# One fused Mamba-and-attention kernel: the scan's state copies and due times, the split of products over the engines, and the last image's end

## The chip, the cores and the metric

The kernel runs on one core of one Trainium2 chip. The metric is the device time of one execution in microseconds (us); the median over several executions is compared. A core has five engines with queues of their own, which wait for each other by semaphores: TensorE (PE, matrix products and transposes; PEld is its weight load), VectorE (DVE), ScalarE (ACT), GpSimd (POOL) and SyncE (SP, which here only issues DMAs). SBUF is the on-chip memory of 128 partitions, PSUM the accumulator memory that PE writes; POOL's operands here all lie in SBUF.

## What is computed

Two layers over x of shape 4 x 512 x 32 x 32 (float32), each after a group normalization and added to its input:

```python
# layer 0, per image: L = 1024 tokens, d_inner = 1024, 16 states
xn = layernorm(tokens(gn(x))) * ln_w + ln_b
xm, z = split(xn @ W_in)
xs = silu(causal_conv4(xm) + conv_b)
proj = xs @ W_x                          # 32 dt columns, 16 B, 16 C
dt = softplus(proj[..., :32] @ W_dt + b_dt)
def step(h, inp):
    dA = jnp.exp(dt_t[..., None] * A)
    h = dA * h + (dt_t * x_t)[..., None] * B_t[:, None, :]
    y = jnp.einsum('bds,bs->bd', h, C_t)
    return (h, y)
x1 = x + ((scan(step) + xs * D_param) * silu(z)) @ W_out
# layer 1, per image, on g = gn(x1)
top, center = conv1x1(g, w_top), conv1x1(g, w_center)     # 64 channels
bottom = conv3x3(g, w_bottom)
att = softmax over all of (center^T top) @ bottom
out = x1 + conv3x3(g + att, w_out)
```

## The kernel before

**Scan stage (layer 0).** The 1024 channels are eight chunks of 128 (`d`), the 1024 tokens two halves of 512 (`h`). For each image `b`, each pair of chunks `e` and each half `h` there are 16 *units*, one for each state `s`: 4 x 4 x 2 x 16 = 512 units. A unit (`unit`, L726 and behind) does, for its two chunks `j`:

- exp(dt * A) on ACT (L746), the *decay*;
- dt * x * B. For the states of `B_ON_ACT` ACT scales the transposed dt * x by B (four instructions of 128 x 256, L758, into a tile `sc`, two buffers) and PE turns it back into PSUM (L784, eight transposes, into a tile `u`, four buffers). For the others POOL multiplies 128 x 1024 by a row of B that SP has broadcast (`bbc`, L767 and L773);
- the recurrence along 512 tokens as one DVE scan for each chunk (L798), from `carry_sb` in the second half;
- in the first half a copy of the last column into `carry_sb`. For the states of `C_ON_DVE`, whose scan writes PSUM, it is inside the scan's step, one number per partition (L803). For the others it is a step of its own behind both scans, two numbers per partition from SBUF (L820);
- the product with C: on POOL, both chunks at once, in place (L826), or on DVE for `C_ON_DVE` (L814), by a row of C that SP has broadcast (`cbc`, L739, six buffers);
- the sum over states: PE transposes the product into PSUM, accumulating (L833).

At the end of 16 units comes a gate (L856 to L876). Between the units lie: for the next image the normalization, the projections with four-tap convolution (`pxm`; L601 on ACT, L610 on DVE), `params` (x times W_x, 16 matmuls, L652) and `delta` (dt, dtx L710 and its transpose); the gates' projections `pz`; the output projection `po`, which writes x1 to DRAM; and 32 transforms of the 3 x 3 convolution weights for layer 1, on POOL and ACT, which fill gaps.

**What sets the order.** All steps of layer 0 are handed to `Plan`. A step has an engine, an estimated time and a due time `prio`, counted in units (one image is 128 units). `Plan.issue` plays the steps through on estimated clocks: among the steps of an engine that could start within `SLACK` of the earliest, it takes the one with the least due time, and no step further than `AHEAD` units in front of the oldest one left. The result is the fixed instruction order of each engine. `PRM` holds the due times: `m0`, `n0`, `nl` normalization of the next image, `q0`/`qg` start and step of its eight x projections for the second image and `c0`/`cg` for later ones, `p0` params, `dl` how far ahead of its units a delta is due, `e0`/`eg` and `g0`/`gg` gates, `o0`/`og` output projection, `t0`/`tg` weight transforms, `fi` the first image's load for layer 1.

**Layer 1.** Not planned by hand: the framework's scheduler orders it. For each image: `scores`, the first 3 x 3 convolution (`conv3`, called b), `attend`, which adds the attention to the padded image `xg`, the second `conv3` (called o) and `finish`. `conv3` takes its weights from DRAM in 24 pieces of 1 MB (L1385, three buffers) through 192 matmul instructions (L1389), in three pairs of points; each point takes four products q = 2, 1, 0, 3. ACT and DVE combine them into `n` (L1397, L1405), and POOL adds `n` to `y[0]` and `y[3]` behind the last pair (L1409, L1410). `finish` loads x1 (L1463, three buffers), turns y back on PE (L1470), adds on DVE (L1475) and stores (L1480). The two bias rows `brow` are loaded and scaled on ACT at the start of layer 1 (L1195, L1198). In the last image the first pair's input of conv o is made chunk by chunk inside `attend`.

Of the kernel before, what the change touches and what calls it, by code (L numbers as in the profile page):

```python
# [29 lines left out]

PRM = dict(fi=4.61, m0=27.7, n0=50.77, nl=1.39, q0=50.1, qg=7.76, c0=53.17, cg=7.07, p0=120.48, e0=6.38, eg=3.72, g0=78.98, gg=9.04, o0=14.48, og=4.13, dl=9.01, t0=10, tg=21.42)

# [23 lines left out]
class Plan:  # L56
# [4 lines left out]
    LAG = {"PE": 0.2, "DVE": 0.08, "ACT": 0.1, "POOL": 0.06, "SP": 0.0}  # L61
    HOP, LOAD, SLACK, AHEAD = 0.05, 1.3, 0.05, 17.64

# [106 lines left out]
def mamba_then_pab_kernel(  # L170
# [46 lines left out]
    nc.gpsimd.dma_start(pb_sb[PAB:P], b_center)  # L217

    def padded(b, pool, tag):

        xg = pool.tile([P, NCC, HH + 2, WW + 2], F32, tag=tag, name=f"xg_{b}")
        nc.gpsimd.memset(xg[:, :, 0, :], 0.0)
        nc.gpsimd.memset(xg[:, :, HH + 1, :], 0.0)
        nc.gpsimd.memset(xg[:, :, 1 : HH + 1, 0], 0.0)
        nc.gpsimd.memset(xg[:, :, 1 : HH + 1, WW + 1], 0.0)
        return xg
# [37 lines left out]
    with ExitStack() as l0:  # L264
# [12 lines left out]

        B_ON_ACT = (0, 2, 4, 6, 7, 8, 10, 12, 14, 15)

        C_ON_DVE = (1, 6, 11)  # L280

# [39 lines left out]
        def dram_set(name, shape, n=B):  # L321
# [7 lines left out]
        slots = {  # L329
            "xt": 1, "xs": 10, "win": 2, "yt": 1, "dt": 2, "dtx": 2, "dtxt": 2, "cbc": 6,  # L330
            "sc": 2, "h": 4, "sz": 1, "bb": 3, "dbx": 4, "szl": 1, "wpr": 2, "res": 2,
# [28 lines left out]
        bts = [buf(None, bt_sb[k], "") for k in range(2)]  # L360
        carry = [buf(None, None, "") for s in range(NS)]
        bcds = [buf(None, t, "") for t in bcd]
# [280 lines left out]
        def params(b, prio):  # L643

            p0 = b % 2 * NP
            pr = proj[b % 2]
            for h, hs in enumerate(halves):
                pp = buf("mm" if b else f"y{h}", [P, T], f"pp_{b}_{h}")
                for d in range(NDC):
                    step(  # L650
                        "PE", MM,
                        lambda d=d, hs=hs, pp=pp: nc.tensor.matmul(  # L652
                            pp()[p0 : p0 + NP, :], wx_sb[:, d, :], xs[b, d]()[:, hs],
                            start=(d == 0), stop=(d == NDC - 1),
                        ),
                        [xs[b, k] for k in range(NDC)] if b and d == 0 else [xs[b, d]], [pp],
                        prio if b else prio - 10 + d + 0.5,
                    )
                step(
                    "ACT", 0.48,  # L660
                    lambda hs=hs, pp=pp: nc.scalar.copy(pr()[:, hs], pp()[p0 : p0 + NP, :]),
                    [pp], [pr], prio,
                )
            step(
                "SP", 0.3, lambda: nc.sync.dma_start(bcd[b], pr()[RK:NP, :]),
                [pr], [bcds[b]], prio, kb=128,
            )
            pt = buf("mm", [P, NT, NP], f"pbt_{b}")

            def turn():  # L670
                for k in range(NT):
                    nc.tensor.transpose(
                        pt()[:, k, :], pr()[:, k * P : (k + 1) * P],
                        ident[p0 : p0 + NP, p0 : p0 + NP],
                    )

            step("PE", 8 * TR, turn, [pr], [pt], prio)
            bt = bts[b % 2]
            step(
                "DVE", 0.21, lambda: nc.vector.tensor_copy(bt(), pt()[:, :, RK : RK + NS]),  # L680
                [pt], [bt], prio,
            )
# [45 lines left out]
        def unit(b, e, h, s, y):  # L728
# [15 lines left out]
            def decay(j, t):  # L744
                at = (2 * e + j) * NS + s
                nc.scalar.activation(t, dt()[:, j], AF.Exp, scale=a_sb[:, at : at + 1])  # L746
# [31 lines left out]
            for j, u in enumerate(us):  # L778
                part = parts[j]
                if on_act:  # L780

                    def turn(j=j, u=u):
                        for k in range(NK):
                            nc.tensor.transpose(  # L784
                                u()[:, k * P : (k + 1) * P], sc()[:, k, j, :], ident
                            )

                    step(
                        "ACT", EXP, lambda j=j: decay(j, hc()[:, j]), [dt], [part], prio, "exp",
                        holds=[hc],  # L790
                    )
                    step("PE", 4 * TR, turn, [sc], [u], prio - 1)
                else:
                    step("ACT", EXP, lambda j=j, u=u: decay(j, u()), [dt], [u], prio - 1, "exp")

                def scan(j=j, u=u):
# [4 lines left out]
                    )  # L801
                    if h == 0 and on_dve:
                        nc.vector.tensor_copy(carry_sb[:, j, s : s + 1], ht[:, T - 1 : T])  # L803

                before, behind = ([carry[s]], []) if h else ([], [carry[s]] if on_dve else [])
                step(
                    "DVE", SCAN + (0.15 if behind else 0.0), scan,
                    [part if on_act else hc, u, *before],
                    [u if on_dve else part, *behind], prio - 1, holds=[hc],
                )  # L810
                if on_dve:
# [4 lines left out]
                    )  # L816
            if h == 0 and not on_dve:
                step(
                    "DVE", 0.15,
                    lambda: nc.vector.tensor_copy(carry_sb[:, :, s], hc()[:, :, T - 1]),  # L820
                    parts, [carry[s]], prio - 1, holds=[hc],
                )
            if not on_dve:
# [5 lines left out]
            for j in range(2):  # L829
# [8 lines left out]

                step("PE", 4 * TR, add, [parts[j]], [y[j]], prio, holds=[hc])

# [149 lines left out]
        def first_image(prio):  # L990
# [10 lines left out]

            step("POOL", 1.2, make, [], [pieces, *chunks], prio)
            for c in range(NCC):
                for h in range(NH):
# [6 lines left out]
                        ),  # L1011
                        [x1s[0][h]], [chunks[c]], prio, kb=512,
                    )
# [161 lines left out]
    with ExitStack() as l1:  # L1175
# [14 lines left out]


        brow = []
        for name, src in (("b", b_bottom), ("o", b_out)):
            t = wp.tile([1, C], F32, tag=f"brow_{name}", name=f"brow_{name}")
            nc.scalar.dma_start(  # L1195
                t.rearrange("o (c p) -> o c p", p=P), src.rearrange("p (c o) -> o c p", o=1)
            )
            nc.scalar.activation(t, t, AF.Copy, scale=2.0 / ALPHA[1])  # L1198
            brow.append(t)
        NMC = L // P  # L1200
# [116 lines left out]

        def conv3(name, xg, u, bias, first=None):

# [46 lines left out]
            for pair in PAIRS:  # L1366
# [14 lines left out]
                for k, p in enumerate(pair):  # L1381
                    m = {}
                    for q in (2, 1, 0, 3):
                        w = fp.tile([P, NCC, C], F32, tag="u", name=f"uw_{name}_{p}_{q}", bufs=3)
                        nc.sync.dma_start(w, u[q][p])  # L1385
# [13 lines left out]
                    for o, src, w, add, op in (  # L1399
# [5 lines left out]
                        nc.vector.scalar_tensor_tensor(o, src, w, add, ALU.mult, op)  # L1405
                    ns.append(n)

                if pair == (0, 5):
                    nc.gpsimd.tensor_add(y[0], y[0], ns[0])  # L1409
                    nc.gpsimd.tensor_add(y[3], y[3], ns[1])  # L1410
                    break
                a, d = (
# [17 lines left out]
        def attend(b, xg, st, rp, xb, between, chunk):  # L1430


            for k in range(NCC * NH):
# [20 lines left out]
                if h and chunk:  # L1454
                    chunk(j)

        def finish(b, y):

            dst = out[b].rearrange("(c p) h w -> p c (h w)", p=P)
            for j in range(NCC):  # L1460
                o = fp.tile([P, L], F32, tag="f4", name=f"o_{b}_{j}")
                for h in range(NH):
                    nc.sync.dma_start(  # L1463
                        o[:, h * T : (h + 1) * T], x1[b][h][j * P : (j + 1) * P, :]
                    )
                ov = o.rearrange("p (i r j k) -> p r k i j", r=4, j=TJ, k=2)
                for rr in range(2):
                    pt = ps.tile([P, 4, P], F32, tag="ps", name=f"po_{b}_{j}_{rr}")
                    for k in range(4):
                        nc.tensor.transpose(  # L1470
                            pt[:, k, :], y[2 * rr + k // 2][:, k % 2, j * P : (j + 1) * P], ident
                        )
                    for k in range(2):
                        o2 = ov[:, 2 * rr + k]
                        nc.vector.tensor_add(  # L1475
                            o2, o2, pt[:, 2 * k : 2 * k + 2].rearrange(
                                "p k (i j) -> p k i j", j=TJ
                            ),
                        )
                nc.scalar.dma_start(dst[:, j, :], o)  # L1480

        xg = image[0]
        st, rp = scores(0, xg)
        for b in range(B):
# [5 lines left out]
            attend(b, xg, st, rp, xb, after, chunk)  # L1490
            if b + 1 < B:
                st, rp = scores(b + 1, image[b + 1])
            finish(b, conv3(f"o{b}", xg, uo, brow[1], v))
            xg = image.get(b + 1)
# [57 lines left out]
```

## Time and profile before

| | us |
|---|---|
| median of 3 runs | 3147.45 (3142.55 to 3149.4) |
| the profiled execution | 3152.2 |
| its span | 3150.4 |

| engine | busy us in the span | share |
|---|---|---|
| PE | 2801.1 | 89% |
| DVE | 2324.9 | 74% |
| ACT | 1896.9 | 60% |
| POOL | 2185.6 | 69% |

The scan stage runs from about 120 to 2096 us, layer 1 from about 2123 to the end. The shares over the whole span mix the two: layer 1 uses POOL and ACT little. In group lines the columns are line, engine, operation, what is written from what, shape and count, then busy us and the mean ns of one, then the engine's idle time in front of them and who ended it. In a timeline line they are start and length in us, engine, line, operation, and in brackets the idle time in front. A window line has the stretch, its length, and for each engine the busy us and the number of instructions.

### The profile page before, as it was taken

To read this page: it belongs to the slowest core of one execution; us is meant where nothing else is said; L and a number is where in the kernel's file an instruction comes from. 1 tells how busy PE (TensorE), PEld (TensorE's weight loads), DVE (VectorE), ACT (ScalarE), POOL (GpSimd) and SP (SyncE) were. 2 spreads that over 40 slices of the span, in tenths; PEclk is the share of its full clock that TensorE was granted. 3 is DMA by queue.
4 is the path that set the end of the run, shared out by engine and by line. 5 is a ranking of instruction groups with operands and counts; after the bars stand their busy time and mean duration, and the time that the engine had idled before them with its cause. 6 is when DMAs were issued, how large, how long until landed. Compare 5 with 4: busy or idle time off the path is not lost. (4 is left out here: it accounts for less than half of the span.)

```text
span 3150.4 us, 36613 instructions
## 1 busy us (share of the span) xinstructions
PE 2801.1 (89%) x11832; PEld 1654.8 (53%) x11832; DVE 2324.9 (74%) x2746; ACT 1896.9 (60%) x3322; POOL 2185.6 (69%) x1207
## 2 busy tenths in 40 slices
PE   4988878989888999888999877779999999999998
PEld 2455656666556656565655655544444444444443
DVE  3488899988999988999987987876275366447344
ACT  3499889998799999789998787752030030020000
POOL 8899898999969999978899998853052142224222
PEclk8999899999999999999999989989999999999999
DMA  6666455577645567745567654457268448628817
GB/s 190 192 186 195 144 152 162 156 226 241 212 118 169 163 204 250 231 114 155 165 192 227 204 172 123 121 139 263 93 225 312 183 147 317 257 74 312 321 61 253
DMA packets 401414, 600.03 MB, mean 190 GB/s; under 512 B 47176, under 2 KB 241992, under 8 KB 376648
## 3 DMA queue, kind: packets, MB, share of 16 engines
q1 hardware_dynamic: 392128, 582.13, 58.8%
q10 hardware_dynamic: 8936, 15.31, 1.3%
q8 instruction: 94, 1.54, 0.2%
q14 instruction: 96, 0.79, 0.1%
q0 software_dynamic: 160, 0.26, 0.0%
HBM read 500.60 MB, written 96.99 MB: 190 GB/s over the span
## 5 line engine op out<-in xcount | busy, mean ns | idle before, releaser
L826 POOL TENSOR_TENSOR da<-da,cbc 128x1024 f32<-128x1024 f32 x288 | 679.4, 2364 | 87.2 <-DVE carry_sb L820 47.4
L758 ACT ACTIVATE sc<-dtxt,bt_sb 128x256 f32<-128x256 f32 x1280 | 557.1, 496 | 49.3 <-PE u L784 48.8
L746 ACT ACTIVATE da<-dt,a_sb 128x512 f32<-128x512 f32 x640 | 439.4, 713 | 70.1 <-PE y L833 69.5
L773 POOL TENSOR_TENSOR dbx<-dtx,bbc 128x1024 f32<-128x1024 f32 x192 | 452.1, 2367 | 30.6 <-DMA bbc<-bcd 8.3
L784 PE MATMUL u<-ident,sc 128*128 128x128 f32 x2560 | 380.6, 282 | 52.4 <-DVE da L798 31.7
L833 PE MATMUL y<-ident,da 128*128 128x128 f32 x2560 | 357.3, 283 | 70.7 <-POOL da L826 68.2
L798 DVE TENSOR_TENSOR_SCAN da<-da,carry_sb,u 128x512 f32<-128x512 f32 x288 | 353.3, 1260 | 82.8 <-PE u L784 82.6
L833 PEld LDWEIGHTS y<-ident,da 128*128 128x128 f32 x2560 | 297.6, 145 | 183.4 <-POOL da L826 134.2
L784 PEld LDWEIGHTS u<-ident,sc 128*128 128x128 f32 x2560 | 302.2, 144 | 160.3 <-issue 41.7
L798 DVE TENSOR_TENSOR_SCAN da<-da,u 128x512 f32<-128x512 f32 x288 | 337.1, 1202 | 37.3 <-PE u L784 37.2
L1389 PE MATMUL m_b<-uw_b,v_b 128*128 128x512 f32 x768 | 339.1, 599 | 10.3 <-DMA uw_b<-u_b 9.4
L1389 PE MATMUL m_o<-uw_o,v_o 128*128 128x512 f32 x768 | 333.5, 595 | 4.3 <-DVE v_o L1311 4.1
L826 POOL TENSOR_TENSOR dbx<-dbx,cbc 128x1024 f32<-128x1024 f32 x128 | 302.8, 2365 | 32.1 <-DVE carry_sb L820 22.6
L381 PE MATMUL pxm<-xt,winc 128*128 128x344 f32 (+2 forms) x768 | 249.6, 469 | 30.5 <-DVE xs L610 13.9
L746 ACT ACTIVATE u<-dt,a_sb 128x512 f32<-128x512 f32 x384 | 252.9, 679 | 34.8 <-DVE da L798 18.9
L833 PE MATMUL y<-ident,dbx 128*128 128x128 f32 x1536 | 217.1, 281 | 43.7 <-POOL dbx L826 31.6
L381 PE MATMUL pz<-xt,winc 128*128 128x512 f32 x512 | 246.2, 599 | 10.5 <-ACT sz L631 3.1
L1389 PEld LDWEIGHTS m_b<-uw_b,v_b 128*128 128x128 f32 x768 | 144.7, 191 | 197.8 <-issue 185.7
L1389 PEld LDWEIGHTS m_o<-uw_o,v_o 128*128 128x128 f32 x768 | 145.5, 190 | 190.5 <-issue 181.2
L833 PEld LDWEIGHTS y<-ident,dbx 128*128 128x128 f32 x1536 | 178.4, 144 | 98.2 <-POOL dbx L826 48.6
L1437 PE MATMUL pat<-y_b,st 128*128 128x512 f32 x512 | 221.7, 593 | 0.1
L1397 ACT ACTIVATE e_b<-m_b 128x512 f32<-128x512 f32 x24 | 14.3, 596 | 320.6 <-PE m_b L1389 299.4
(231 smaller groups left out, 4536.2 us busy)
## 6 DMA issues: line engine op xcount, KB each, us to landing
cbc<-bcd SPq DMA_DIRECT2D x512, 256.0 KB, 3.7
uw_b<-u_b SPq DMA_DIRECT2D x96, 1024.0 KB, 4.9
uw_o<-u_o SPq DMA_DIRECT2D x96, 1024.0 KB, 4.9
bbc<-bcd SPq DMA_DIRECT2D x192, 256.0 KB, 4.1
u_b<-work SPq DMA_DIRECT2D x192, 128.0 KB, 2.3
u_o<-work SPq DMA_DIRECT2D x192, 128.0 KB, 3.1
winc<-in_w_in_dram SPq DMA_DIRECT2D x64, 256.0 KB, 3.8
szd<-sz SPq DMA_DIRECT2D x32, 512.0 KB, 3.6
```

The lines of the kernel that those rows point to most:

```text
L381: lambda k=k, lhs=lhs, rhs=rhs: nc.tensor.matmul(p()[:, at : at + cols], lhs(), rhs(), start=(k == 0), stop=(k == n - 1)),
L746: nc.scalar.activation(t, dt()[:, j], AF.Exp, scale=a_sb[:, at : at + 1])
L758: nc.scalar.activation(sc()[:, k], dtxt()[:, k], AF.Copy, scale=bt()[:, at, s : s + 1])
L773: lambda: nc.gpsimd.tensor_mul(hc(), dtx(), b_bc().to_broadcast([P, 2, T])),
L784: nc.tensor.transpose(u()[:, k * P : (k + 1) * P], sc()[:, k, j, :], ident)
L798: nc.vector.tensor_tensor_scan(ht, *((hc()[:, j], u()) if on_act else (u(), hc()[:, j])), carry_sb[:, j, s : s + 1] if h else 0.0, ALU.mul ...
L826: lambda: nc.gpsimd.tensor_mul(hc(), hc(), c_bc().to_broadcast([P, 2, T])),
L833: nc.tensor.matmul(y[j]()[:, k, :], hc()[:, j, k * P : (k + 1) * P], ident, start=(s == 0 and k == 0), stop=(s == NS - 1 and k == NK - 1), ...
L1389: nc.tensor.matmul(m[q], v[:, q, k, c, :], w[:, c, :], start=(c == 0), stop=(c == NCC - 1 and not extra),)
L1397: nc.scalar.activation(e, m[2], AF.Copy, scale=al / 2)
L1437: nc.tensor.matmul(pt, st[m][:, 2 * P * j + h : 2 * P * (j + 1) : 2], xb[m // 2][:, m % 2, :], start=(m == 0), stop=(m == NMC - 1),)
```

## The change

In the scan stage the copy of the state is made in each scan's step, one number per partition, for every state. `B_ON_ACT` loses state 7 (nine states on ACT), `C_ON_DVE` becomes (1, 5, 9, 13) from (1, 6, 11). The turns L784 are due two units ahead (`kt`), the accumulating transposes L833 0.68 units later (`ka`), the 16 params matmuls one every 0.53 units from 112 (`pg`, `p0`), and other due times move; `ke` and `fl` have the values that leave things as they were. `cbc` has five buffers instead of six. The bias rows are loaded and scaled at the program's start, from a pool that lives through the program. In layer 1 the last addition to y[0] and y[3] goes in halves, each behind its own point; in the last image the four x1 chunks are loaded into the scores' buffers ahead of conv o, y's first two rows (r = 0, 1) are turned and added before the last product, y[3]'s last addition is on DVE, and the stores go out over two queues.

```diff
-PRM = dict(fi=4.61, m0=27.7, n0=50.77, nl=1.39, q0=50.1, qg=7.76, c0=53.17, cg=7.07, p0=120.48, e0=6.38, eg=3.72, g0=78.98, gg=9.04, o0=14.48, og=4.13, dl=9.01, t0=10, tg=21.42)
+PRM = dict(pg=0.53, kt=2, ke=1, ka=-0.68, fl=0, fi=4.6, m0=45.7, n0=50.77, nl=2.05, q0=65.56, qg=5.2, c0=61.67, cg=6.03, p0=112, e0=3.46, eg=4.75, g0=78.98, gg=9.04, o0=13.03, og=5.23, dl=10.28, t0=11, tg=21.42)
...
-    HOP, LOAD, SLACK, AHEAD = 0.05, 1.3, 0.05, 17.64
+    HOP, LOAD, SLACK, AHEAD = 0.05, 1.3, 0.07, 17.64
...
+    brow = []
+    for name, src in (("b", b_bottom), ("o", b_out)):
+        t = cpool.tile([1, C], F32, tag=f"brow_{name}", name=f"brow_{name}")
+        nc.scalar.dma_start(
+            t.rearrange("o (c p) -> o c p", p=P), src.rearrange("p (c o) -> o c p", o=1)
+        )
+        nc.scalar.activation(t, t, AF.Copy, scale=-12.0)
+        brow.append(t)
...
-        B_ON_ACT = (0, 2, 4, 6, 7, 8, 10, 12, 14, 15)
-        C_ON_DVE = (1, 6, 11)
+        B_ON_ACT = (0, 2, 4, 6, 8, 10, 12, 14, 15)
+        C_ON_DVE = (1, 5, 9, 13)
...
-            "xt": 1, "xs": 10, "win": 2, "yt": 1, "dt": 2, "dtx": 2, "dtxt": 2, "cbc": 6,
+            "xt": 1, "xs": 10, "win": 2, "yt": 1, "dt": 2, "dtx": 2, "dtxt": 2, "cbc": 5,
...
-                        prio if b else prio - 10 + d + 0.5,
+                        prio + PRM["pg"] * (d + NDC * h) if b else prio - 10 + d + 0.5,
...
-                    step("PE", 4 * TR, turn, [sc], [u], prio - 1)
+                    step("PE", 4 * TR, turn, [sc], [u], prio - PRM["kt"])
...
-                    if h == 0 and on_dve:
+                    if h == 0:
                         nc.vector.tensor_copy(carry_sb[:, j, s : s + 1], ht[:, T - 1 : T])
...
-            if h == 0 and not on_dve:
-                step(
-                    "DVE", 0.15,
-                    lambda: nc.vector.tensor_copy(carry_sb[:, :, s], hc()[:, :, T - 1]),
-                    parts, [carry[s]], prio - 1, holds=[hc],
-                )
...
-                step("PE", 4 * TR, add, [parts[j]], [y[j]], prio, holds=[hc])
+                step("PE", 4 * TR, add, [parts[j]], [y[j]], prio - PRM["ka"], holds=[hc])
...
+                        if late and (p, q) == (5, 3):
+                            late(y)
...
+                    if pair == (0, 5):
+                        eng = nc.vector if late and k else nc.gpsimd
+                        for c in range(2):
+                            eng.tensor_add(y[3 * k][:, c], y[3 * k][:, c], n[:, c])
                 if pair == (0, 5):
-                    nc.gpsimd.tensor_add(y[0], y[0], ns[0])
-                    nc.gpsimd.tensor_add(y[3], y[3], ns[1])
                     break
...
+        def last(b, xg, v):
+
+            o = [load_sum(b, j, xp, "st") for j in range(NCC)]
+
+            def late(y):
+                for j in range(NCC):
+                    turn_back(b, j, o[j], y, 0)
+
+            y = conv3(f"o{b}", xg, uo, brow[1], v, late)
+            for j in range(NCC):
+                turn_back(b, j, o[j], y, 1)
+                (nc.scalar, nc.sync)[j % 2].dma_start(dst[b][:, j, :], o[j])
```

`load_sum` is the two x1 loads of a chunk, `turn_back(b, j, o, y, rr)` four transposes and two additions for two of the four rows; both are cut out of `finish`.

## The prediction

> **What bounds it now.** I read the page, then busy time by stage, then the groups by line and shape, the waits, and last the timeline where those pointed. The stages, with the columns PE, PEld, DVE, ACT and POOL busy, granted clock, DMA share and GB/s:
>
> ```profile
> 120.00:2096.00 1976.00, 1709.59 (x9188) 1162.43 (x9187) 1734.72 (x2049) 1703.19 (x2999) 1780.45 (x962) 0.96 0.60 178
> 2096.00:2123.00 27.00, 19.36 (x45) 8.43 (x44) 9.93 (x20) 10.01 (x17) 6.13 (x4) 0.78 0.29 95
> 2123.00:3133.70 1010.70, 988.36 (x2357) 439.27 (x2358) 525.33 (x568) 139.04 (x241) 292.93 (x130) 0.99 0.61 218
> 3133.70:3150.40 16.70, 4.58 (x33) 3.27 (x31) 6.16 (x17) 0.00 (x0) 2.36 (x1) 0.76 0.42 157
> ```
>
> The scan stage (1976 us) has four engines within 86 to 90% of its length; POOL is the fullest, idle for 195.5 us. The last stage before the tail is PE's: 98% busy at a clock of 0.99, so only its ends can move. The 27 us between the stages and the 16.7 us behind the last matmul are chains, not work. What POOL waits for in the scan:
>
> ```profile
> L826 POOL TENSOR_TENSOR da<-da,cbc 128x1024 f32<-128x1024 f32 x288 | 679.4, 2364 | 87.2 <-DVE carry_sb L820 47.4 <-DVE da L798 20.2 <-PE u L784 4.5
> L826 POOL TENSOR_TENSOR dbx<-dbx,cbc 128x1024 f32<-128x1024 f32 x128 | 302.8, 2365 | 32.1 <-DVE carry_sb L820 22.6 <-POOL dbx L773 2.3 <-POOL da L826 1.6
> L820 DVE COPY carry_sb<-da 128x2 f32<-128x2 f32 x144 | 83.8, 582 | 3.9
> L820 DVE COPY carry_sb<-dbx 128x2 f32<-128x2 f32 x64 | 43.3, 676 | 1.6
> L803 DVE COPY carry_sb<-u 128x1 f32<-128x1 f32 x96 | 15.2, 158 | 3.3
> L814 DVE TENSOR_TENSOR dbx<-u,cbc 128x512 f32<-128x512 f32 x128 | 84.0, 670 | 0.0
> L758 ACT ACTIVATE sc<-dtxt,bt_sb 128x256 f32<-128x256 f32 x1280 | 557.1, 496 | 49.3 <-PE u L784 48.8
> L784 PE MATMUL u<-ident,sc 128*128 128x128 f32 x2560 | 380.6, 282 | 52.4 <-DVE da L798 31.7 <-ACT sc L758 9.2 <-DVE dbx L798 7.1
> ```
>
> 70.0 us of POOL's idle time ends with the state copy of L820. That copy moves two numbers per partition from SBUF and takes 582 to 676 ns on the mean, though its shortest is 156; the copy of one number from PSUM (L803) takes 158 always. Two lines of the timeline say why: the copy starts while POOL works and ends when POOL ends.
>
> ```profile
> 1304.50 2.35 DVE L820 COPY carry_sb<-da 128x2 f32<-128x2 f32 x1
> ...
> 1304.46 2.36 POOL L773 TENSOR_TENSOR dbx<-dtx,bbc 128x1024 f32<-128x1024 f32 x1
> ```
>
> But a wait that ends with the copy is not always the copy's. In the longest of them the copy took 0.17 us, and it was the scan in front of it that was late, behind convolution taps (L610) on DVE:
>
> ```profile
> 1391.79 1.21 DVE L798 TENSOR_TENSOR_SCAN da<-da,u 128x512 f32<-128x512 f32 x1
> 1393.03 0.17 DVE L820 COPY carry_sb<-da 128x2 f32<-128x2 f32 x1
> ...
> 1393.43 2.36 POOL L826 TENSOR_TENSOR da<-da,cbc 128x1024 f32<-128x1024 f32 x1 [7.47 <-DVE carry_sb L820]
> ```
>
> **The change, scan stage: work moved.** One state's B product leaves ScalarE and PE for POOL: 32 units. ACT loses 128 scalings of 557.1/1280 = 0.435 us, 55.7 us. PE loses 256 turns of 380.6/2560 = 0.149, 38.1 us. POOL gains 32 products of 2.367 (L773) and loses 32 of 2.364 (L826), because one more state's C product goes to DVE: POOL stays as it is. DVE gains 64 products of 0.670, 42.9 us. SP issues 32 more row loads of 256 KB, 8.4 MB, against 352 MB that the stage moves (178 GB/s by 1976 us); its DMA share is 0.60, so I cost them at nothing; without that cover one would cost its 4.1 us to landing.
>
> **The copies.** Before: 208 of two numbers (127.1 us) and 96 from PSUM (15.2). After: 12 states times 16 first halves times 2, 384 copies of one number from SBUF, and 128 from PSUM. The trace has no copy of one number from SBUF. Lower bound: the PSUM row, 0.158, so 60.7 us; DVE then has 42.9 + 60.7 + 5.1 - 127.1 = 18.4 us less to do. Upper bound: each is held like the 2.35 us one; a random start in a POOL product of 2.36, POOL being 90% busy, leaves 1.18 x 0.90 = 1.06, with its own 0.16 1.22 us, 468 us in all. I take the lower: the shape is that of L803 but for where it reads. This is the widest open term.
>
> The Trainium skill, SBUF — State Buffer, "Who interferes with whom", says that a VectorE copy in a two-port mode and a GpSimd instruction exclude each other for a whole instruction; the 2.35 us row agrees. VectorE: DVE Perf Modes, "What auto-detection actually checks", gives the mode to one-source operations within SBUF when the outermost dimension that is not one is even, or equal on both sides. It speaks against the change if one element counts as odd and equal: then the sum goes by the upper bound. One element has no such dimension, so the page leaves it open, and no row here shows it.
>
> **What POOL's idle time gives back** (the stage's end follows POOL, whose work is the same). Carry waits: 70.0 us in 50 waits. With the copy inside the scan's step nothing gets between scan and copy, and a copy no longer waits on POOL; but the scan may be late itself. Ends 0 and -70; I take a third, -22, because the longest cases look like the one above. Waits on the scan itself, 20.2: DVE waits 119.8 us for turned u (42 times, one of 20.8 at the start); turns due two units ahead and 38 us less on PE shorten that, but with two sc and four u buffers not by much: ends 0 and -20, taken -8. The products dtx wait 26.7 us for ACT's dt (6 times); delta due 1.27 units earlier is 1.27 x 1976/512 = 4.9 us, and ACT has less to do: ends 0 and -26.7, taken -8. cbc with five buffers instead of six: one unit, 3.86 us, less lead for loads that land in 3.7; behind a late one SP holds the B rows and weights too, and POOL waits for those. Ends 0 and +8.3 (what POOL's products wait for B rows now), taken +3. The later and denser start of the x projections (53.17 to 61.67 units, step 7.07 to 6.03) moves 8.5 units, 33 us, and no instruction; the spread x-parameter matmuls end where they did, at 112 + 16 x 0.53 = 120.48. These open POOL's worst gap somewhere else:
>
> ```profile
> 1388.10:1459.70 71.60, 62.40 (x319) 43.99 (x320) 64.34 (x89) 62.99 (x106) 47.42 (x23) 0.95 0.47 132
> ```
>
> There, in the half-scan in which the taps begin, POOL is busy for 47.4 of 71.6. Moving the taps can win or lose some 10 us for each of two such places: ends -20 and +20, taken 0. Sum of the scan: -22 - 8 - 8 + 3 = **-35**, ends +28 and -137.
>
> **Between the stages.** ACT waits for the bias rows' DMA, and the root of the first image's variance is queued behind it:
>
> ```profile
> 2099.20 1.24 ACTq L1195 DMA_DIRECT2D brow_b<-in_b_bottom_dram  x1
> ...
> 2105.18 0.63 ACT L1198 ACTIVATE brow_b<-brow_b 1x512 f32<-1x512 f32 x1 [8.55 <-DMA brow_b<-in_b_bottom_dram]
> 2105.83 1.28 ACT L245 ACT_TABLE_LOAD   x1
> ```
>
> Its input was there at 2101.2 (matmul L1045, 2100.88 + 0.28). Loaded at the program's start, the rows free ACT: 2105.83 - 2101.2 = **-4.6**, and PE, DVE and the scores behind it move along. At the start ACT has nothing on the chain before 25.42; the two DMAs of 4-byte pieces share the engines with xt, which starts PE at 20.61: 0 to +3, taken **+1**.
>
> **Tail.** Now: last matmul 3133.7, n 0.9, POOL's addition to y 2.36, transposes and eight additions of DVE in 2.74 us, three stores, then
>
> ```profile
> 3145.41 1.41 DVE L1475 TENSOR_TENSOR o<-o,po 128x256 f32<-128x256 f32 x4 [5.17 <-DMA o<-x]
> ```
>
> with the fourth x1 chunk waiting for a buffer. After: n 0.9, half of y on DVE 0.67, transposes 0.5, two additions 0.7 (2.74/8 each), first store at +2.8; four stores of 512 KB at 321 GB/s (the best slice) 6.5, and 1.9 around a store (3.5 to landing less its own 1.6): +11.2 against 16.7. Ahead of the last four matmuls go 16 transposes of 16.8/128 = 0.131 us, +2.1, on a full PE. Together **-3.4**, ends 0 and -6. The eight x1 loads now stand before the weights on SP's queue and reuse the scores' buffers, free only when attention ends; loads have been issued out of program order here (a uw_b at 2116.71 before the last x of L984), so I cost it at nothing.
>
> **Sum.** -35 - 4.6 + 1 - 3.4 = -42. The profiled execution took 3152.2 (span 3150.4 and 1.8 around it), 4.75 over the median of 3147.45; the differences are taken off the median: **3105**. Own range 3050 (the scan at two thirds of its best end) to 3140 (the scan unmoved).
>
> **Rivals.**
> 1. *DVE is held by POOL at every copy* (slower). Place: the 16 first halves. DVE's 1734.7 becomes 1734.7 + 42.9 + 5.1 - 127.1 + 468 = 2124, over the stage's 1976: at least +148 full, +260 at 95%. As POOL idles more the holds shorten, so +170: 3147 - 7 + 170 = 3310. It decides once a copy costs more than (1976 - 1734.7 + 127.1 - 48)/384 = 0.83 us. For it: the 2.35 us row. Against: the 158 ns row of the same size.
> 2. *Only the ends move*: POOL's waits change their names, since its 1780 us of work are the same. For it: the 0.17 us copy behind a late scan. 3147.45 - 7 = 3140, up to 3150 if the new due times cost 10.
> 3. *x1 blocks the weights*: eight loads of 256 KB wait on SP until attention ends; 2.1 MB and the first weights (1 MB) at 300 GB/s take 10.5 us against a present PE gap of 4 to 5. +6 on the forecast: 3111, and it can't carry the sign.
>
> **Chances.** Forecast 0.63 (rival 3 inside it, at 0.08), rival 2 0.20, rival 1 0.13, something else slower 0.04. A measurement tells 0.2%, 6.3 us, from no change, so faster means under 3141.2. Rival 2 lies on that line and gives 0.11 to faster, 0.08 to same and 0.01 to slower. Faster 0.74, same 0.08, slower 0.18. Low 3050 is the forecast's own low end; high 3165 takes in rival 2 with the scan near its worst end (3147 - 7 + 25); rival 1 is left out.
>
> **What would show it.** L803 or L820's successor at about 160 ns and nowhere tied to POOL's ends; POOL's idle time in the scan near 160 us, with "carry_sb" gone and scans in its place; ACT some 56 and PE some 38 us less; no wait on brow at the change of stage; the last o loaded before the tail, and stores back to back. Wrong if copies average over 0.8 us, if DVE passes POOL in the scan, or if waits on cbc and bbc grow by over 20 us.

## The result

| | median us | ratio to before, 95% interval |
|---|---|---|
| before | 3148.4 (4 runs) | |
| changed | 3103.4 (3102.9 to 3107.6, 4 runs) | 0.9859 (0.9835 to 0.9882) |

45 us faster; the forecast was 3105. Time by stage in the changed kernel, with the columns of the windows shown before (length, then PE, PEld, DVE, ACT and POOL busy, clock, DMA share, GB/s):

```profile
120.00:2065.60 1945.60, 1695.04 (x8934) 1156.61 (x8933) 1723.41 (x2322) 1664.36 (x2878) 1777.34 (x963) 0.95 0.62 185
2065.60:2086.90 21.30, 18.39 (x45) 8.82 (x44) 9.73 (x20) 8.94 (x16) 6.22 (x4) 0.82 0.34 122
2086.90:3091.40 1004.50, 987.30 (x2374) 440.20 (x2375) 526.78 (x578) 139.02 (x241) 293.96 (x145) 1.00 0.62 220
3091.40:3101.50 10.10, 2.10 (x16) 1.42 (x14) 4.11 (x10) 0.00 (x0) 0.00 (x0) 0.79 0.52 208
```

Against 1976.0, 27.0, 1010.7 and 16.7: the scan stage is 30.4 us shorter, the gap between the stages 5.7, layer 1 6.2, the tail 6.6. POOL's work in the scan is the same (1780.4 and 1777.3), so its idle time is what shrank, from 195.6 to 168.3 us. Now what POOL waits for, and the copies: the source view of the C product (idle time in front of it, us and times, by what ended it), then that of the copy (shortest, median, longest in ns), then the group of the dtx products, changed and before:

```profile
  DVE carry_sb L815: 56.9, 34
  DVE da L810: 41.1, 27
  issue: 7.7, 6
  DVE dbx L810: 5.4, 6
...
L815 DVE COPY carry_sb<-da x288: 152/154/156, 167.0 to 2002.8; 128x1 f32<-128x1 f32 x144
L815 DVE COPY carry_sb<-u x128: 157/158/160, 169.7 to 1995.2; 128x1 f32<-128x1 f32 x128
L815 DVE COPY carry_sb<-dbx x96: 153/154/156, 176.2 to 1988.7; 128x1 f32<-128x1 f32 x96
...
L722 POOL TENSOR_TENSOR dtx<-dt,xs 128x512 f32<-128x512 f32 x64 | 80.2, 1277 | 4.1 <-ACT dt L714 4.0
...
L710 POOL TENSOR_TENSOR dtx<-dt,xs 128x512 f32<-128x512 f32 x64 | 80.2, 1277 | 26.7 <-ACT dt L702 26.7
```

No copy of one number is held: 152 to 160 ns, wherever it reads. But POOL's waits on DVE have not become fewer. Those that end with the copy went from 70.0 to 56.9 us, those that end with a scan (of `da` or `dbx`) from 21.7 to 46.5, together from 92 to 103. Since the copy now takes 0.15 us right behind its scan, both names say the same thing: the scan was late. What shrank is elsewhere, the wait for ACT's dt before the dtx products (26.7 to 4.0) the most.

The root of the first image's variance no longer stands behind a bias row. ACT's timeline at the change of stage:

```profile
2066.22 1.28 ACT L255 ACT_TABLE_LOAD   x1
2071.83 0.26 ACT L255 ACTIVATE grstd_image<-pv_image,eps 128x4 f32<-128x4 f32 x1 [4.33 <-PE pv_image L1051]
2072.11 1.28 ACT L256 ACT_TABLE_LOAD   x1
```

The table is loaded while ACT waits for PE, so that its 1.28 us leave the chain too. And the tail, DVE's and the stores' timelines:

```profile
3091.38 0.69 DVE L1405 SCALAR_TENSOR_TENSOR n_o<-m_o,n_o 128x512 f32<-128x512 f32 x1 [1.22 <-PE m_o L1389]
3092.11 0.69 DVE L1410 TENSOR_TENSOR y_o<-y_o,n_o 128x512 f32<-128x512 f32 x1
3093.22 2.74 DVE L1480 TENSOR_TENSOR o<-o,po 128x256 f32<-128x256 f32 x8 [0.42 <-PE po L1475]
...
3094.66 1.66 SPq L1503 DMA_DIRECT2D out_dram<-o  x2
...
3094.01 1.66 ACTq L1503 DMA_DIRECT2D out_dram<-o  x2
```

Behind the last `n`, POOL's addition of 2.36 us has become half an addition of 0.69 us on DVE, no addition waits for an x1 chunk, and the four stores start within 2.3 us.

### The profile page after: what moved, and what is told of

Same layout as the page of the kernel before. It is cut to its first block, busy times and chain, and to the rows that moved or that the text cites. A ratio compares the mean times of both kernels' runs of the same rounds, so it can differ in the third digit from the quotient of the medians.

```text
span 3101.5 us, 36237 instructions
## 1 busy us (share of the span) xinstructions
PE 2779.4 (90%) x11576; PEld 1647.4 (53%) x11576; DVE 2312.2 (75%) x3020; ACT 1858.1 (60%) x3201; POOL 2180.3 (70%) x1221
## 4 chain that ended last, share of the span: by engine, by line
PE 37%; DVE 12%; ACT 4%; DMA 3%; issue 2%; POOL 2%; SPq 0%; DVEq 0%; POOLq 0%; ACTq 0%
PE m_o L1389 10%; PE m_b L1389 9%; PE pat L1439 7%; DVE da L810 4%; PE y L839 2%; DVE u L810 2%; PE po L391 2%; PE psc L1266 2%; DVE dbx L810 2%; DMA uw_b<-u_b 1%; PE u L796 1%; ACT sc L770 1%; DVE dbx L826 1%; PE pt L1245 1%; PE pz L391 1%
## 5 line engine op out<-in xcount | busy, mean ns | idle before, releaser
L832 POOL TENSOR_TENSOR da<-da,cbc 128x1024 f32<-128x1024 f32 x288 | 680.3, 2368 | 96.8 <-DVE carry_sb L815 52.4
L785 POOL TENSOR_TENSOR dbx<-dtx,bbc 128x1024 f32<-128x1024 f32 x224 | 528.5, 2369 | 23.5 <-PE y L839 5.8
L770 ACT ACTIVATE sc<-dtxt,bt_sb 128x256 f32<-128x256 f32 x1152 | 503.7, 497 | 62.1 <-PE u L796 61.2
L758 ACT ACTIVATE da<-dt,a_sb 128x512 f32<-128x512 f32 x576 | 394.5, 713 | 47.6 <-PE y L839 44.6
L796 PE MATMUL u<-ident,sc 128*128 128x128 f32 x2304 | 350.9, 286 | 56.0 <-DVE da L810 38.2
L839 PE MATMUL y<-ident,da 128*128 128x128 f32 x2304 | 323.9, 286 | 54.2 <-POOL da L832 49.5
L758 ACT ACTIVATE u<-dt,a_sb 128x512 f32<-128x512 f32 x448 | 297.3, 680 | 49.2 <-DVE da L810 30.4
L839 PE MATMUL y<-ident,dbx 128*128 128x128 f32 x1792 | 268.8, 289 | 52.6 <-POOL dbx L832 26.0
L839 PEld LDWEIGHTS y<-ident,dbx 128*128 128x128 f32 x1792 | 218.6, 149 | 128.5 <-POOL dbx L832 49.2
L832 POOL TENSOR_TENSOR dbx<-dbx,cbc 128x1024 f32<-128x1024 f32 x96 | 227.2, 2367 | 19.3 <-issue 7.4
L620 DVE SCALAR_TENSOR_TENSOR xs<-pxm,cw_sb,xs 128x341 f32<-128x341 f32 (+4 forms) x288 | 163.7, 570 | 49.2 <-ACT xs L611 42.0
```

Source lines behind the costliest of these rows:

```text
L620: nc.vector.scalar_tensor_tensor(u()[:, first:end], p()[:, first - k - at + before : end - k - at + before], cw[k], u()[:, first:end], ALU ...
L770: nc.scalar.activation(sc()[:, k], dtxt()[:, k], AF.Copy, scale=bt()[:, at, s : s + 1])
L785: lambda: nc.gpsimd.tensor_mul(hc(), dtx(), b_bc().to_broadcast([P, 2, T])),
L796: nc.tensor.transpose(u()[:, k * P : (k + 1) * P], sc()[:, k, j, :], ident)
L832: lambda: nc.gpsimd.tensor_mul(hc(), hc(), c_bc().to_broadcast([P, 2, T])),
L839: nc.tensor.matmul(y[j]()[:, k, :], hc()[:, j, k * P : (k + 1) * P], ident, start=(s == 0 and k == 0), stop=(s == NS - 1 and k == NK - 1), ...
```

## The experiments

Each median stands beside runs of the kernel before on the same chip (3147.3 to 3147.6, for the changed kernel 3148.4). The *stage* is the length of the scan stage from 120 us to the last gate's start, with DVE's busy time in it, from one profile each.

| run | copy | split | due times | median us | ratio (95%) | stage | DVE busy |
|---|---|---|---|---|---|---|---|
| changed | own step | new | new | 3103.4 | 0.9859 (0.9835 to 0.9882) | 1945.6 | 1723.4 |
| e1 | merged | new | new | 3137.9 | 0.9969 (0.9957 to 0.9980) | 1980.5 | 1770.5 |
| e2 | own step | old | new | 3112.4 | 0.9888 (0.9874 to 0.9903) | 1954.0 | 1688.9 |
| e3 | own step | new | old | 3142.8 | 0.9985 (0.9974 to 0.9996) | 1987.0 | 1726.4 |
| e4 | merged | old | old | 3132.2 | 0.9951 (0.9934 to 0.9968) | 1978.2 | 1735.3 |
| e6 | own step | old | old | 3130.8 | 0.9939 (0.9923 to 0.9956) | 1976.8 | 1688.9 |
| e10 | merged | old | new | 3151.0 | 1.0010 (0.9999 to 1.0021) | 1990.3 | 1736.8 |
| e5 | own step, two wide | new | new | 3273.2 | 1.0398 (1.0383 to 1.0414) | 2114.0 | 1922.7 |

"Own step" is the copy in each scan's step, "merged" the step of its own behind both scans. All of these have the new ends and five cbc buffers. One more input of the planner goes with the due times in e4 and e6: the estimated size of one load for layer 1, 512 KB as before instead of 768. In e3 it stays at 768.

**e1, the merged copy in the changed kernel.**

```diff
-                    if h == 0:
+                    if h == 0 and on_dve:
...
+            if h == 0 and not on_dve:
+                step(
+                    "DVE", 0.15,
+                    lambda: nc.vector.tensor_copy(carry_sb[:, :, s], hc()[:, :, T - 1]),
+                    parts, [carry[s]], prio - 1, holds=[hc],
+                )
```

> The changed kernel with one edit undone: the copy of the state is again a step of its own, two numbers per partition, for the states that are not in C_ON_DVE. Theory C (the copy gave the scan its gain: DVE no longer held by POOL, nothing between scan and copy): loses 20 us or more against the changed kernel, so about 3125 to 3135, and the copies take 0.5 us or more on the mean. Theory S (the new split of products, which relieves ACT and PE) and theory D (the due times): within 8 us of the changed kernel's 3103, though the copies are held.

34.5 us lost: theory C's sign, 3 us beyond its range, and the copies are held again:

```profile
L832 DVE COPY carry_sb<-da 128x2 f32<-128x2 f32 x144 | 89.1, 619 | 3.2
L832 DVE COPY carry_sb<-dbx 128x2 f32<-128x2 f32 x48 | 27.3, 569 | 1.2
```

**e2, the old split in the changed kernel.**

```diff
-        B_ON_ACT = (0, 2, 4, 6, 8, 10, 12, 14, 15)
-        C_ON_DVE = (1, 5, 9, 13)
+        B_ON_ACT = (0, 2, 4, 6, 7, 8, 10, 12, 14, 15)
+        C_ON_DVE = (1, 6, 11)
```

> The changed kernel with B_ON_ACT and C_ON_DVE of the kernel before (ten states on ACT, three on DVE). Theory S: 20 us or more are lost, 3123 and over, with ACT busy for 56 us more and waits on ACT up. Theories C and D: within 8 us of 3103, because POOL's work is the same 19 products per half.

9.0 us lost, a little over what the other theories allowed and under half of theory S's: in the changed kernel the split is the smallest of the three.

**e3, the old due times in the changed kernel.**

```diff
-PRM = dict(pg=0.53, kt=2, ke=1, ka=-0.68, fl=0, fi=4.6, m0=45.7, ...
-    HOP, LOAD, SLACK, AHEAD = 0.05, 1.3, 0.07, 17.64
+PRM = dict(pg=0, kt=1, ke=1, ka=0, fl=0, fi=4.61, m0=27.7, ...
+    HOP, LOAD, SLACK, AHEAD = 0.05, 1.3, 0.05, 17.64
```

> The changed kernel with every due time of the kernel before (PRM and SLACK; turns one unit ahead, params at one time, additions not delayed). Theory D: 20 us or more are lost, 3123 and over, and POOL's wait for dt before the products dtx is back from 4 to some 27 us. Theories C and S: within 8 us of 3103.

39.4 us lost: theory D's number as well; the wait for dt came back only to 15 us. Two of three theories that were meant to exclude each other both held, each with more than the 30.4 us that the scan stage had gained. So parts were put on, one at a time, from the other side.

**e4, the kernel before with the new ends.** The changed kernel with copy, split, due times and SLACK of the one before.

> The kernel before with the ends of the changed one alone: bias rows loaded at the start, cbc with five buffers, the last additions to y in halves, x1 ahead and rows in parts in the last image; copy, split and due times as before. By the sum of the prediction -7 us, 3141. By the two traces (17.0 to 11.2 us between the stages, 1010.6 to 1004.5 in layer 1, 16.7 to 10.1 in the tail) -18 us, 3130, less what the fifth cbc buffer costs (0 to 8).

-15.4 us, nearer to the traces' number than to the prediction's. Its one profile fell on the slowest of its five executions (3126 to 3140, the profile 3139.8), so that the stage's 2.2 us more can't be told from none. The start, too, varies between executions: PE's first matrix product comes at 25.8 us here and at 23.1 to 26.7 in the other profiles with early bias rows, against 20.6 in the one profile before; the first scan comes at 171.2 here, at 165.0 to 172.3 in the others and at 166.2 before.

**e6, e4 with the copy in each scan's step.**

> The kernel of e4 (before with the new ends, 3132) with the state copy in each scan's step; split and due times as before. Theory C as a mechanism of its own (DVE is freed whatever the due times are): 10 us or more gained, under 3122. Theory I (copy and due times gain only together, since the order is made from both): within 8 us of 3132 or slower.

-1.4 us, within the intervals (some 5 us each way) nothing. The two windows of the scan stage, e4 and then e6:

```profile
120.00:2098.20 1978.20, 1711.48 (x9203) 1160.22 (x9202) 1735.28 (x2055) 1705.12 (x3005) 1786.33 (x967) 0.97 0.60 178
```

```profile
120.00:2096.80 1976.80, 1723.70 (x9199) 1180.37 (x9198) 1688.93 (x2261) 1708.17 (x3008) 1779.70 (x965) 0.95 0.60 178
```

DVE lost 46.4 us of work and held time, and the stage did not move.

**e10, e4 with the new due times and SLACK.**

> The kernel of e4 (before with the new ends, 3132) with the new due times and SLACK; copy as a step of its own and split as before. With e1, e2, e4 and e6 it closes the square of copy and due times at the old split. Theory I (they gain only together): within 8 us of 3132. If the due times gain alone: under 3122.

Neither expectation: 18.8 us slower than e4. With copies in their steps the same due times gain 18.4 us (e6 to e2).

**e5, copies of two numbers in each scan's step.** This puts a price on rival 1 of the prediction: instructions and due times as in the changed kernel, only the copy's width differs.

```diff
-        carry_sb = wp.tile([P, 2, NS], F32, tag="carry", name="carry_sb")
+        carry_sb = wp.tile([P, 2, NS, 2], F32, tag="carry", name="carry_sb")
...
-                        carry_sb[:, j, s : s + 1] if h else 0.0, ALU.mult, ALU.add,
+                        carry_sb[:, j, s, 1:2] if h else 0.0, ALU.mult, ALU.add,
...
-                        nc.vector.tensor_copy(carry_sb[:, j, s : s + 1], ht[:, T - 1 : T])
+                        nc.vector.tensor_copy(carry_sb[:, j, s], ht[:, T - 2 : T])
```

> The changed kernel with each state copy two numbers wide (the last two columns into a pair of places; the scan reads the second), order and all else the same. Rival 1 of the prediction priced this at +170 us if copies are held by POOL until its product ends (0.8 us or more each): 3270 or more, with DVE the fullest engine of the scan. If two numbers are held only as they were before (0.6 us on the mean, since DVE and POOL run in step): 384 x 0.45 = 170 us more on DVE, of which half shows, 3190. If the width makes no difference: 3103.

169.8 us over the changed kernel. The time is the first expectation's, but the hold is nearer to the second's: 0.69 us a copy, 199.3 us more on DVE, of which 0.85 shows in the stage instead of half. In the scan stage all engines have their instructions in the same order in both traces, so the copy's width is all that differs. The same five instructions in both, DVE and then POOL; first e5:

```profile
1225.34 0.58 DVE L815 COPY carry_sb<-da 128x2 f32<-128x2 f32 x1
1225.83 1.21 DVE L810 TENSOR_TENSOR_SCAN dbx<-u,dbx 128x512 f32<-128x512 f32 x1
1227.07 1.35 DVE L815 COPY carry_sb<-dbx 128x2 f32<-128x2 f32 x1
...
1223.49 2.40 POOL L785 TENSOR_TENSOR dbx<-dtx,bbc 128x1024 f32<-128x1024 f32 x1
1226.05 2.35 POOL L832 TENSOR_TENSOR da<-da,cbc 128x1024 f32<-128x1024 f32 x1 [0.16 <-DVE carry_sb L815]
```

and the changed kernel:

```profile
1140.91 0.15 DVE L815 COPY carry_sb<-da 128x1 f32<-128x1 f32 x1
1140.99 1.22 DVE L810 TENSOR_TENSOR_SCAN dbx<-u,dbx 128x512 f32<-128x512 f32 x1
1142.25 0.15 DVE L815 COPY carry_sb<-dbx 128x1 f32<-128x1 f32 x1
...
1139.47 2.39 POOL L785 TENSOR_TENSOR dbx<-dtx,bbc 128x1024 f32<-128x1024 f32 x1
1141.79 2.40 POOL L832 TENSOR_TENSOR da<-da,cbc 128x1024 f32<-128x1024 f32 x1
```

In e5 the first copy ends at 1225.92, POOL's product at 1225.89; the second at 1228.42 and 1228.40. In the changed kernel the copies run through POOL's products. In e5 230 of the 384 copies from SBUF take over 0.25 us, and each of the 230 ends within 0.08 us of the end of a POOL instruction; the longest, 4.28 us, is held through two in a row. The copies from SBUF take 692 and 671 ns on the mean in e5, those of the same width from PSUM still 159:

```profile
L815 DVE COPY carry_sb<-da 128x2 f32<-128x2 f32 x288 | 199.3, 692 | 10.0
L815 DVE COPY carry_sb<-dbx 128x2 f32<-128x2 f32 x96 | 64.4, 671 | 3.3
L815 DVE COPY carry_sb<-u 128x2 f32<-128x2 f32 x128 | 20.3, 159 | 4.4
...
L815 DVE COPY carry_sb<-da x288: 168/505/4278, 170.0 to 2172.1; 128x2 f32<-128x2 f32 x144
```

**e7 and e8, which due times.** e7 has `kt=1, ka=0`, e8 the old `m0, nl, q0, qg, c0, cg`.

> The changed kernel with the turns due one unit ahead instead of two and the accumulating transposes not delayed. If these two due times carry the 39 us of e3: 3130 or more, with DVE's waits for PE's turned u up from 96.8 to 120 us. If the projections' due times carry it: within 8 us of 3103.

> The changed kernel with the old due times of the next image's normalization and x projections (m0, nl, q0, qg, c0, cg) and nothing else undone. If they carry the 39 us of e3: 3130 or more, lost in the first three images. If the turns do: within 8 us of 3103.

e7 3122.4 (0.9920, 0.9905 to 0.9935), +19.0; e8 3134.7 (0.9955, 0.9940 to 0.9970), +31.3, most of it in the first two images (by the last gate of each image: end of the first 651.7 to 663.1, length of the second 483.0 to 493.0). Both count, the projections more; but the two losses add up to 50.3, more than the 39.4 of e3, so they are no shares of a sum either. The wait that e7 was to bring back did not come: DVE's waits for turned u fell from 96.8 to 79.8 us. So why the earlier turns help is not shown.

**e9, due times nudged.** `q0` and `c0` 0.1 units later, `dl` 0.02 more.

> The changed kernel with the x projections due 0.1 units (0.4 us) later and delta 0.02 units earlier: no mechanism is touched, only the places at which the planner breaks near ties. Theory M (due times have a mechanism, the time varies smoothly with them): within 6 us of 3103. Theory L (the due times are a lucky fit to one order): 10 us or more slower, and the size of e7 and e8 says little of turns or projections as such.

3104.6 (0.9863, 0.9848 to 0.9878): theory M's number. The order did change, but little (DVE's differs in 90 of the 2350 instructions of the first 2000 us), so the gain is not a stroke of luck at exactly one point of the due times; how far around it holds was not tried.

**e11, two states fewer on DVE in the last two halves.**

```diff
-            on_act, on_dve = s in B_ON_ACT, s in C_ON_DVE
+            tail = b == B - 1 and 2 * e + h >= 6
+            on_act, on_dve = s in B_ON_ACT, s in (C_ON_DVE, (1, 9))[tail]
```

> The changed kernel with only states 1 and 9 in C_ON_DVE in the last two halves of the last image, where POOL is busy for 70 and 79% and DVE for 93 and 89%. 4 x 2 x 0.67 = 2.7 us less on DVE in each, 2 x 2.36 us more on POOL, which has 15 and 12 us idle: -3 to -5 us, 3099. If the order there is no longer set by DVE: 3103 or slower.

3102.0 (0.9861, 0.9845 to 0.9876): not to be told from the changed kernel, so neither expectation is shown.

**e12, whole additions to y in layer 1.**

```diff
+                        if late:
                             for c in range(2):
                                 eng.tensor_add(y[3 * k][:, c], y[3 * k][:, c], n[:, c])
                 if pair == (0, 5):
+                    if not late:
+                        nc.gpsimd.tensor_add(y[0], y[0], ns[0])
+                        nc.gpsimd.tensor_add(y[3], y[3], ns[1])
                     break
```

> The changed kernel with the last additions to y[0] and y[3] whole and behind both points again, except in the last image's conv o. The two traces put 1.2 us on each of three joints between conv o and the next conv b (7.4 against 6.2 us), and 1 to 2 us on the joints behind conv b: +4 to +6 us, 3108. If the halves do nothing there: 3103.

3106.0 (0.9866, 0.9851 to 0.9881): +2.6 us, less than the runs can tell. The timeline of PE at the first joint (where the last products of one image's conv o meet the next image's conv b) shows what the halves do. e12, then the changed kernel:

```profile
2347.11 1.02 PE L1389 MATMUL m_b<-uw_b,v_b 128*128 128x512 f32 x2
2349.41 1.31 PE L1479 MATMUL po<-ident,y_o 128*128 128x128 f32 x10 [1.27 <-POOL y_o L1415]
2350.56 1.88 PE L1389 MATMUL m_b<-uw_b,v_b 128*128 128x512 f32 x4
```

```profile
2349.03 1.02 PE L1389 MATMUL m_b<-uw_b,v_b 128*128 128x512 f32 x2
2350.14 1.20 PE L1475 MATMUL po<-ident,y_o 128*128 128x128 f32 x9
2351.18 1.88 PE L1389 MATMUL m_b<-uw_b,v_b 128*128 128x512 f32 x4
```

PE's 1.27 us of waiting for POOL's whole addition are gone. There are three such joints, as the waits of the kernel before and of e12 have it (us in total, times, longest; before, the fourth is in the tail). The changed kernel has no such wait:

```profile
PE po L1470 <- POOL y_o L1410: 5.1, 4, 1.3
...
PE po L1479 <- POOL y_o L1415: 3.8, 3, 1.3
```

## Why the prediction was right, and where it was not

**The total and the sign** held: 3105 against 3103.4, inside the forecast's own range. Its two halves were off by some 5 to 10 us each, and against each other, so that the 2 us between forecast and result are luck. By the runs the 45 us are 15.4 for the ends (before to e4), 19.8 for copy and due times together (e4 to e2) and 9.0 for the split on top of them (e2 to changed).

**The copies' bound** was chosen rightly. One number per partition takes 154 ns from SBUF too, the lower end. But the reason given, the 158 ns row of L803, could not decide it: that row reads PSUM, and in e5 a copy of two numbers from PSUM takes 159 ns as well. So the row says nothing of the width, and to that extent the choice was luck. Rival 1's +170 us came out as +169.8 in e5 by chance too: it had 1.22 us a copy and 2124 us of DVE, and e5 has 0.69 us and 1922.7. Its threshold, 0.83 us a copy, fell: at 0.69 the loss is already whole. It assumed that nothing is lost until DVE is full, but DVE's busy share in e5's stage is 91%.

**"What POOL's idle time gives back"** is the step that failed. Its sum, -35, is near the stage's -30.4, and the stage did follow POOL's idle time (27.3 us less), but the terms under it are not what happened. It gave -30 to POOL's waits on copy and scan, which grew by 12. Its next term, -8, was for dtx, which gave 22.7; neither this -8 nor the +3 behind it is worked out there, and 1.27 x 1976/512 is 4.9, not 4. No run shows the +3. Above all it added the copy (-22) and the later projections ("taken 0") as if each worked alone. The square at the old split, all with the new ends, shows that they do not:

| median us | old due times | new due times |
|---|---|---|
| copy merged | 3132.2 (e4) | 3151.0 (e10) |
| copy in the scan's step | 3130.8 (e6) | 3112.4 (e2) |

Alone the copy gives nothing and the due times lose 19; together they gain 20. The split is bound up with them too: e3 and e6 differ in the split and in the one load's estimate, and there, under the old due times, the new split is 12.0 us slower (3142.8 against 3130.8). The table of stages says what the copy's part depends on. Merged to own step takes 46 to 48 us of busy time from DVE each time. Under the old due times the stage follows by 1.4 us (e4 to e6), under the new ones by 36.3 (e10 to e2) and 34.9 (e1 to the changed kernel); and e5's 199.3 us more on DVE lengthen it by 168.4. So under the new due times a microsecond of DVE costs 0.74 to 0.85 us of the stage, under the old ones 0.03. The reading that fits is that the new due times make an order that DVE paces, and that only there is it worth anything that DVE is no longer held. It is argued, not shown: only e5 keeps the order of the instructions (0.85, and there POOL waits longer for the copies as well, 157.9 us instead of 56.9); in the other pairs the planner made a new order, and no wide copy was tried in the order of e6. That the planner had the merged copy down for 0.15 us, where it takes about 0.6, fits with the loss in e10, but no run separates that. Nor was it tried whether due times searched anew for the merged copy would reach the same.

**The split** moved nearly what was worked out: ACT's scalings fell from 557.1 to 503.7 us (53.4, forecast 55.7) and PE's turns from 380.6 to 350.9 (29.7, forecast 38.1), with POOL unchanged. The stage's busy time fell by less, ACT's by 38.8 and PE's by 14.6, so that sign of the forecast did not come. Under the new due times the split is worth 9 us (e2), a term that the sum had nowhere.

**The ends** were mis-sized, -7 against -15.4 in e4. Right: the tail, +11.2 forecast and 10.1 measured behind the last matmul, and the transposes ahead of the last product, +2.1 against 1.8 (conv o of the last image from its first unbroken row to its end, 75.8 to 77.6). Too small: the gap between the stages by the hidden table load (-4.6 forecast, 5.7 measured). The start, taken +1, is 2.5 to 6.1 us at PE's first product and -1.2 to 6.1 at the first scan, by profile and against the one profile before; the changed kernel's has 4.1 and -0.5. Left out: the three joints of layer 1, 3.8 us of PE's waits; the change's halves were costed for the last image alone. Of the rest of layer 1's difference, 2.0 us are fewer waits for the 1 MB weight loads (9.4 to 7.4); this rest is within what varies, since layer 1 takes from 1003.6 to 1009.0 us in the profiles that share the changed kernel's layer 1.

**Rival 2**, only the ends, is what e4 and e6 are, at 3131 to 3132 instead of 3140, and not the changed kernel. **Rival 3** did not occur: the first weights of conv o were there, and PE's wait for the last chunk's input is the same 4.09 us as before.

## What to carry to other kernels

In a stage where several engines are 86 to 90% busy, as here, do not book gains to waits one by one: undo each part in the new kernel and put each on the old one. Here two parts were each worth more than the stage's whole gain when undone, and put on alone one gave nothing and the other a loss. Idle time named after an instruction belongs to everything in front of it on its engine, so a wait that keeps its size under a new name has not been removed. And due times belong to one set of steps: change the steps, and the old ones are a different schedule, not a neutral one.

## What the runs showed of the hardware

A VectorE copy within SBUF waits for a running GpSimd product when it moves two numbers per partition (692 and 671 ns on the mean, up to 4.3 us, in e5) and not when it moves one (152 to 156 ns in 384 of 384, in the changed kernel). The Trainium skill, VectorE: DVE Perf Modes, "What auto-detection actually checks", leaves the case of one element open: it lets a copy within SBUF into a two-port mode when the outermost dimension that is not one is even or equal on both sides. Here the copy of one element is not held as a copy in that mode would be; the mode itself is not seen in a trace. In e5 the two-wide copy from PSUM takes 159 ns. That agrees with the same section, which gives the mode only where source and destination lie in SBUF.
